# A four-layer graph network on one core: matmuls of no use in TensorE's waits at the start, and a new order table

## The chip, the cores and the metric

The kernel runs on one core of a Trainium2 chip. The core's engines work side by side, each through its own queue in order: TensorE (PE; its weight loads are the row PEld), VectorE (DVE), ScalarE (ACT), GpSimd (POOL) and SyncE (SP, which here only issues DMAs). Time is the device's microseconds from launch to end. Of the kernel before there are three timed runs, with a median of 3752.26 us (3751.09 to 3758.95), and one profiled execution.

## The reference

32 graphs, each of N = 512 nodes with D = 256 features in float32 and a symmetric 0/1 adjacency with ones on the diagonal, go through four graph layers. Ahead of each layer stands a norm without weights and a ReLU, around it a residual sum:

```python
for layer in (L0, L1, L2, L3):
    h = maximum(layernorm(x), 0)
    x = x + layer(h, adj)
```

- Layer 0 is graph attention with 4 heads of 64: `Wh = h @ W`, scores `leaky_relu(e_src[i] + e_dst[j])` masked by the adjacency, softmax over j, `alpha @ Wh`, ELU.
- Layer 1 is the same with one head of 256 and a softmax over the other axis.
- Layer 2 has scores `(h * a) @ h.T`, leaky ReLU, mask, softmax, times `h`.
- Layer 3 is a transformer block: q, k and v, 8 heads of 32 under the mask, an output projection, a norm, a feed-forward part of 256 x 1024 x 256 with ReLU, a norm.

## The kernel before, in words

Nodes are laid in four tiles of 128 partitions. All matmuls take float32. The profile shows each of them as two MATMUL rows, and a transpose (a matmul with the identity, L257) as one.

Nothing is written out in the order in which it runs. `quick_path` records each graph's work as jobs: `plan.dve`, `plan.act`, `plan.matmuls`, `plan.dma` (L214, L235, L257 and L259 are the lines that issue them, whatever the stage, so that stages are told apart by the names of tiles). Each job of a graph has a number in the order of recording, and the table `PLACES` holds one place for each number. Job n of graph b stands at

```python
place = self.number * ROUND + self.table[self.at] if self.place is None else self.place
```

with `ROUND` = 100000 as the distance of two graphs. The table reaches up to 491710, so the work of up to five graphs interleaves: while one is in layer 3, the next are in the layers 2, 1 and 0. `carry_out` (L178) sorts all jobs by place and issues them; each engine's jobs are tied together in just this order ("as planned"). An engine thus never passes over a job that waits. One table serves all 32 graphs: at the start, when the graph ahead is missing, its jobs are missing too, and nothing takes their room.

`aside(place)` (L141) gives the jobs that follow a fixed place: the late loads of weights on POOL, and a few one-off steps.

On its way a graph passes these tiles, in TensorE's terms:
- layer 0: transposes of `h` into `ps_t`, `ps_wh` (128x264), the small transpose `ps_sp`, whose result goes to DRAM (`rows_d`) and comes back spread over all partitions (`rows`, 1 MB); then four heads. For each, VectorE makes four `p` (128x512) from `rows`, and TensorE does 16 matmuls of 128x65 into `ps_o`; VectorE then divides (`rt`, `o`). `p` has six buffers.
- layer 1: `ps_t`, `ps_wh` (128x258), `ps_sp`, 16 matmuls of 128x256 (`ps_o1` in the code, `ps_o` in the profile).
- layer 2: `ps_t`, `ps_e`, the transposes `ps_y`, `ps_o2` (128x257).
- layer 3: `ps_t3` (in the profile `ps_t`), `ps_v`, `ps_qk`, then eight rounds of `ps_s` (scores), exp on ScalarE, the product `p` with the mask on VectorE, `ps_ct` and `ps_to`; then `ps_wo`, `ps_t3`, `ps_f1`, `ps_f2` (both `ps_f` in the profile).

The mask of a graph (`m`) is transposed by four DMAs (`mT`). In PSUM the layers 0 to 2 take the two buffers of `ps_a`, layer 3 the two of `ps_b` (two banks each) and `ps_ct`, `ps_to`.

Of the kernel before, what the change touches and what calls it, by code (L numbers as in the profile page):

```python
# [16 lines left out]
OP = mybir.AluOpType  # L17
AX = mybir.AxisListType

P = 128  # L20
# [36 lines left out]
class Part:  # L57


    def __init__(self, home, rows, index, steps=()):  # L60
        self.home, self.rows, self.index, self.steps = home, rows, index, steps
# [61 lines left out]
class Plan:  # L123
# [6 lines left out]
        tensor_copy=(1,), tensor_scalar_max=(1,), tensor_scalar_mul=(1,),  # L130
    )

    def __init__(self, tc, table):
        self.tc, self.nc, self.table = tc, tc.nc, table
        self.jobs = []

    def graph(self, number):

# [11 lines left out]
    def put(self, engine, takes, ends, outs, ins, call, port=False, moves=None):  # L150

        j = Job()
        place = self.number * ROUND + self.table[self.at] if self.place is None else self.place
        j.place = (place, self.at)
        self.at += 1
        j.engine, j.takes, j.ends, j.call, j.port, j.moves = engine, takes, ends, call, port, moves
        j.after, j.homes = [], []
        before = set()
        for part, writes in [(p, True) for p in outs] + [(p, False) for p in ins]:
            h = part.home  # L160
            r0, r1 = int(part.rows.min()), int(part.rows.max())
            i0, i1 = int(part.index.min()), int(part.index.max())
            if in_psum(part):
                i0, i1 = 0, 1 << 20
            for k, w, a0, a1, b0, b1 in h.uses:
                if (w or writes) and k is not j and a0 <= r1 and r0 <= a1 and b0 <= i1 and i0 <= b1:
                    before.add(k)
            h.uses.append((j, writes, r0, r1, i0, i1))
            if h not in j.homes:
                j.homes.append(h)  # L170
                h.left += 1
        for k in before:
            assert k.place < j.place, "out of order"
            k.after.append(j)
        self.jobs.append(j)
        return j
# [61 lines left out]
    def load(self, tile, source, behind):  # L238
# [7 lines left out]

        return self.put("POOL", 1.0, 0.1, [], [], call)

    def matmuls(self, takes, *calls):

        real = lambda x: x.real() if isinstance(x, Part) else x

        def call():
            made = []
            for c in calls:
                if len(c) == 3:
                    made.append(self.nc.tensor.transpose(*map(real, c)))  # L257
                else:
                    made.append(self.nc.tensor.matmul(*map(real, c[:3]), start=c[3], stop=c[4]))  # L259
            return made  # L260

        outs = [c[0] for c in calls]
        ins = [x for c in calls for x in c[1:3] if isinstance(x, Part)]
        return self.put("PE", takes, takes + 0.2, outs, ins, call)
# [6 lines left out]
def in_psum(x):  # L271
    return isinstance(x, Part) and x.home.kind.tag.startswith("ps")


def width(args):
# [4 lines left out]

ROUND = 100000
PLACES = [
    19807, 0, 43241, 57619, 64598, 73580, 81389, 88138, 134062, 235662, 143142, 287307, 285553, 232853, 15635,
    15811, 28841, 27985, 23993, 15811, 30374, 30229, 32369, 32370, 32370, 32446, 32844, 48496, 34324, 44230,
    44177, 46695, 46041, 50344, 54161, 54792, 54792, 54792, 51041, 51777, 57310, 57310, 57310, 57738, 57738,
    57832, 57739, 58104, 61341, 61341, 67966, 61898, 61898, 67567, 69254, 72469, 69482, 77323, 74000, 76325,
    79818, 78024, 78024, 80713, 80713, 80714, 82170, 88138, 93984, 93675, 88138, 100363, 101562, 103520,
    103520, 103520, 103520, 99026, 98456, 107942, 108892, 114155, 115978, 115979, 116955, 117229, 118109,
    112967, 112266, 118498, 118106, 122333, 124077, 124856, 124856, 126720, 126720, 130323, 126361, 126793,
    124647, 132760, 132760, 132760, 132760, 134221, 134221, 134221, 134221, 134221, 134727, 134221, 156322,  # L290
    140191, 134912, 142057, 169073, 157725, 170057, 172384, 201862, 202787, 205641, 207797, 208539, 176096,
    208573, 211867, 216328, 218484, 218484, 219056, 219056, 219056, 219056, 219056, 218484, 218484, 218484,
    218484, 218485, 227052, 227119, 228253, 219613, 219613, 220424, 224906, 224906, 228631, 223683, 224122,
    224122, 229201, 229201, 232797, 231582, 232020, 232794, 233389, 243904, 244480, 249048, 254893, 242125,
    242231, 243790, 254173, 237217, 238008, 241105, 245079, 237839, 238826, 242604, 256707, 257566, 258334,
    259006, 259006, 259006, 259519, 259519, 259519, 259519, 259519, 392456, 255868, 267182, 259006, 259006,
    259892, 259665, 259006, 259006, 259892, 259665, 266786, 266786, 268621, 269711, 273176, 302934, 273176,
    273176, 273176, 277010, 277447, 281097, 281097, 281195, 281196, 281196, 281682, 281682, 281682, 281682,
    281683, 281196, 281683, 282840, 282840, 284327, 283254, 286775, 286821, 286821, 287236, 288036, 287335,
    282681, 282681, 283122, 282681, 284575, 293213, 293213, 295654, 291792, 291574, 293905, 297714, 297584,  # L300
    297714, 298819, 298819, 297714, 287489, 287489, 290592, 290231, 298206, 300033, 308229, 310297, 310297,
    303799, 303799, 303799, 305379, 305380, 306132, 308300, 312883, 316207, 394029, 437737, 327509, 328548,
    327753, 325228, 328998, 329876, 332238, 330645, 332238, 332502, 332502, 332608, 332717, 364575, 332717,
    332717, 332717, 332717, 332717, 338203, 340406, 340406, 340406, 340407, 340407, 340905, 341309, 341309,
    352943, 347109, 352371, 352371, 353369, 353369, 353417, 354661, 356381, 356381, 356381, 357144, 357399,
    346769, 348254, 348493, 351248, 352029, 352189, 352199, 352199, 352554, 359237, 359237, 359237, 359237,
    364034, 360298, 360301, 360448, 365688, 377452, 366095, 368722, 368232, 374829, 379739, 379671, 380891,
    379672, 382370, 383191, 386847, 392755, 392755, 387818, 392756, 395158, 396303, 407857, 382331, 382331,
    382615, 382634, 388690, 385894, 388773, 389314, 389314, 394131, 390806, 394842, 396200, 401293, 405927,
    398693, 403322, 398865, 403593, 407530, 409955, 410479, 412422, 412422, 408793, 409986, 423530, 354795,  # L310
    408893, 410479, 418263, 418263, 418263, 419191, 419191, 419191, 419191, 419128, 417119, 437177, 437347,
    419191, 420203, 420203, 420203, 420203, 420721, 420203, 420203, 421199, 422452, 422452, 423633, 423633,
    432009, 424134, 424134, 424718, 424718, 424759, 425616, 425916, 425916, 425916, 425916, 426698, 426841,
    426841, 426970, 427475, 430939, 430939, 427202, 428368, 428368, 428368, 429763, 429360, 431209, 431243,
    432263, 432263, 432291, 432540, 430070, 430071, 430071, 430071, 430446, 430071, 431829, 432836, 432836,
    435307, 436332, 440746, 435945, 435945, 436252, 436626, 436626, 437927, 444318, 444318, 444811, 444811,
    444811, 445291, 445291, 445291, 445291, 445447, 445572, 436110, 437653, 437653, 437653, 437653, 437653,
    438770, 440843, 440843, 440843, 440843, 440843, 440872, 442233, 442446, 442446, 442446, 445600, 445600,
    442446, 442446, 445601, 445601, 442446, 442704, 446845, 449648, 449758, 449759, 449759, 454221, 449777,
    450699, 450699, 450699, 450699, 450699, 450699, 491710,  # L320
]


# [1 line left out]
def quick_path(  # L325
# [6 lines left out]
    B, N, D = x.shape  # L332
    NT = N // P
    KD = D // P
# [29 lines left out]
    plan = Plan(tc, PLACES)  # L364

    def new(tag, name, shape, dtype=F32):
        return plan.tile(K[tag], name, shape, dtype)


    ident = const.tile([P, P], F32, name="ident")  # L370
# [14 lines left out]
    w0_t = weight_of(nc, const, w0, "w0_t", 2 * H0)  # L385
# [43 lines left out]
    FULL, HALF = 0.858, 0.4315  # L429
# [372 lines left out]
    bv_w, ps = new("p", "bv_w", [P, N]), new("ps_a", "ps_bv", [P, N])  # L802
# [4 lines left out]

    plan.dve("tensor_scalar_add", b2_r, b2_r, -2.0)
    plan.dve("tensor_add", b1_r, b1_r, ff2b_r)


    for b in range(B):
# [504 lines left out]
```

## Time and profile before

| | us |
|---|---|
| median of three runs | 3752.26 |
| the profiled execution | 3758.1 |
| its span, first to last instruction | 3756.2 |
| PE busy | 3635.0 (97%), 19974 rows |
| DVE busy | 2732.6 (73%) |
| ACT busy | 1803.8 (48%) |
| mean granted TensorE clock | 0.976 |

All that follows is read from that one execution. The page's second part cuts the span in 40 slices of 94 us; a digit is a busy share in tenths, and PEclk is the share of the full TensorE clock that the chip granted:

```profile
PE   4799999999999999999999999999999999999996
PEld 4666766666766666666666666666666666666553
DVE  4577777877777777777787777787777777777653
ACT  1245445555444555444555544555544455544543
POOL 1000000000000000000000000000000000000000
PEclk7599999999999999999999999999999999999998
```

The kernel has a fill of some 300 us, a steady part, and a drain of some 330 us. The view of waits says who waited for whom, in how much time, how often, and how long at most. TensorE's longest:

```profile
PE ps_o L259 <- DVE p L214: 24.6, 9, 10.0
PE ps_t L257 <- ACT h L214: 17.6, 2, 14.8
PE ps_t L257 <- ACT n L214: 12.5, 3, 5.0
PE ps_n L1277 <- DVE least L1273: 8.2, 1, 8.2
PE ps_bv L259 <- issue: 7.3, 1, 7.3
PE ps_ct L259 <- DVE p L214: 6.3, 6, 1.3
PE ps_t L257 <- DVE mc L214: 5.7, 1, 5.7
PE ps_sp L257 <- ACT rt L214: 5.5, 5, 1.4
```

### The profile page before, as it was taken

What the parts mean: (1) busy time and instruction counts of PE and PEld (TensorE: products, weight loads), DVE (VectorE), ACT (ScalarE), POOL (GpSimd) and SP (SyncE); (2) the same over time, 40 slices, a digit from 0 to 9 for tenths busy, and PEclk for the clock granted to TensorE, in tenths of its full rate; (3) what the DMA queues carried; (4) which work ended last, traced back from release to release, by engine and by line L of the source; (5) the groups of instructions that cost most, each with busy time, mean ns of one, the idle gap of its engine ahead of it and who ended that gap; (6) DMA issues with size and microseconds to landing.
All of it is one profiled execution on the core that took longest, in us unless ns stands there. A gap on an engine that the chain in (4) does not pass through costs nothing.

```text
span 3756.2 us, 51774 instructions
## 1 busy us (share of the span) xinstructions
PE 3635.0 (97%) x19974; PEld 2366.4 (63%) x19974; DVE 2732.6 (73%) x6267; ACT 1803.8 (48%) x3393; POOL 11.1 (0%) x25
## 2 busy tenths in 40 slices
PE   4799999999999999999999999999999999999996
PEld 4666766666766666666666666666666666666553
DVE  4577777877777777777787777787777777777653
ACT  1245445555444555444555544555544455544543
POOL 1000000000000000000000000000000000000000
PEclk7599999999999999999999999999999999999998
DMA  4111111111111111011111111111111111100000
GB/s 120 57 32 33 36 49 46 43 42 36 29 49 46 43 49 36 23 47 47 49 43 38 40 29 49 46 43 49 29 29 49 46 43 49 38 29 27 15 9 11
DMA packets 152349, 152.72 MB, mean 41 GB/s; under 512 B 87840, under 2 KB 122144, under 8 KB 148000
## 3 DMA queue, kind: packets, MB, share of 16 engines
q1 hardware_dynamic: 149632, 144.35, 13.8%
q0 software_dynamic: 1216, 3.94, 0.3%
q8 instruction: 159, 2.61, 0.3%
q10 hardware_dynamic: 1248, 1.05, 0.1%
q14 instruction: 94, 0.77, 0.1%
HBM read 114.57 MB, written 17.96 MB: 35 GB/s over the span
## 4 chain that ended last, share of the span: by engine, by line
PE 95%; DVE 3%; ACT 1%; DMA 1%; issue 1%; SPq 0%; ACTq 0%; DVEq 0%
PE ps_o L259 25%; PE ps_f L259 24%; PE ps_s L259 7%; PE ps_ct L259 7%; PE ps_wh L259 6%; PE ps_qk L259 6%; PE ps_to L259 6%; PE ps_e L259 4%; PE ps_t L257 4%; PE ps_v L259 3%; PE ps_wo L259 3%; DVE p L214 1%; PE ps_y L257 1%; DVE st L214 0%; DMA mT<-m 0%
## 5 line engine op out<-in xcount | busy, mean ns | idle before, releaser
L259 PE MATMUL ps_o<-wh,p 128*128 128x65 f32 (+1 forms) x5120 | 750.5, 303 | 30.2 <-DVE p L214 24.6
L259 PEld LDWEIGHTS ps_o<-wh,p 128*128 128x128 f32 x5120 | 705.6, 200 | 102.7 <-issue 60.5
L214 DVE TENSOR_TENSOR p<-p,m 128x2048 f32<-128x2048 f32 x256 | 582.7, 2286 | 29.7 <-ACT p L214 29.6
L214 ACT ACTIVATE p<-ps_s 128x1024 f32<-128x1024 f32 x512 | 501.2, 1022 | 208.1 <-PE ps_s L259 205.3
L259 PE MATMUL ps_f<-tT,ff_t 128*128 128x512 f32 x1024 | 462.7, 602 | 1.7 <-ACT tT L214 1.7
L259 PE MATMUL ps_f<-ff_t,f 128*128 128x256 f32 x2048 | 461.0, 379 | 0.0
L259 PEld LDWEIGHTS ps_f<-ff_t,f 128*128 128x128 f32 x2048 | 381.9, 190 | 64.0 <-issue 15.3
L214 DVE SCALAR_TENSOR_TENSOR p<-rows,rt,mT 128x512 f32<-128x512 f32 x512 | 370.1, 735 | 16.7 <-DMA mT<-m 16.7
L214 ACT ACTIVATE h<-x,shift,rstd 128x256 f32<-128x256 f32 x512 | 268.6, 595 | 152.8 <-PE ps_o L259 106.3
L259 PEld LDWEIGHTS ps_f<-tT,ff_t 128*128 128x128 f32 x1024 | 189.4, 192 | 229.3 <-issue 188.7
L259 PE MATMUL ps_s<-qk 32*128 32x512 f32 x2048 | 294.2, 640 | 1.3 <-ACT qk L214 0.8
L259 PE MATMUL ps_ct<-p,v 128*32 128x512 f32 x2048 | 272.0, 603 | 9.3 <-DVE p L214 6.3
L214 ACT ACTIVATE f<-ps_f,ff1b_c 128x512 f32<-128x512 f32 x256 | 164.8, 682 | 235.7 <-PE ps_f L259 235.7
L259 PE MATMUL ps_to<-p,ones 128*32 128x512 f32 x2048 | 266.6, 592 | 0.0
L259 PE MATMUL ps_qk<-h3T,wqkv_t 128*128 128x512 f32 x512 | 239.1, 594 | 0.0
L259 PE MATMUL ps_o<-h,p 128*128 128x257 f32 x1024 | 239.0, 385 | 0.0
L259 PEld LDWEIGHTS ps_o<-h,p 128*128 128x128 f32 x1024 | 190.1, 191 | 51.5 <-issue 26.0
L214 DVE BATCH_NORM_STATS2 st<-x 128x6 f32<-128x256 f32 x512 | 195.6, 415 | 6.8 <-DMA x<-in_x_dram 4.7
L214 ACT ACTIVATE rstd<-mv,eps 128x4 f32<-128x4 f32 x192 | 56.4, 294 | 298.6 <-DVE mv L214 286.0
L257 PE MATMUL ps_t<-ident,h 128*128 128x128 f32 x1024 | 172.6, 281 | 25.0 <-ACT h L214 17.6
L259 PEld LDWEIGHTS ps_s<-qk 32*128 32x128 f32 x2048 | 81.3, 182 | 164.6 <-ACT y L214 78.0
L257 PEld LDWEIGHTS ps_t<-ident,h 128*128 128x128 f32 x1024 | 130.8, 145 | 85.2 <-issue 52.3
(131 smaller groups left out, 4322.9 us busy)
## 6 DMA issues: line engine op xcount, KB each, us to landing
adj<-in_adj_dram SPq DMA_DIRECT2D x32, 1024.0 KB
rows<-rows_d SPq DMA_DIRECT2D x32, 1024.0 KB
x<-in_x_dram SPq DMA_DIRECT2D x32, 512.0 KB
rows<-rows_d SPq DMA_DIRECT2D x32, 512.0 KB
out_dram<-y SPq DMA_DIRECT2D x32, 512.0 KB
inv<-in_d SPq DMA_DIRECT2D x32, 256.0 KB
ff_t<-in_L_gnn_W_dram POOLq DMA_DIRECT2D x2, 1024.0 KB, 12.5
mT<-m SPq DMA_TRANSPOSE x128
```

The costliest lines, as they stand in the source:

```text
L214: return [getattr(unit, method)(*map(real, args), **{k: real(v) for k, v in kw.items()})]
L257: made.append(self.nc.tensor.transpose(*map(real, c)))
L259: made.append(self.nc.tensor.matmul(*map(real, c[:3]), start=c[3], stop=c[4]))
```

## The change

A new list `WARM` holds 17 places, each with a number of products, 78 in all. At each of these places a job of TensorE is put in, which multiplies the identity with 256 columns of a weight, again and again, into a tile `ps_warm` of the kind `ps_b`. Nothing reads the tile. By their places they stand around the work of the first graph in the layers 0 to 2 (and that of the graphs 1 and 2 in layer 0): 15 ahead of graph 0's heads of layer 0, then 3, 4 and 3 between these heads, 8 ahead of graph 1's first transposes, 16 ahead of graph 1's heads and 3 between its first two, and the rest ahead of graph 2's transposes and `ps_wh`, and around `ps_e` and `ps_y` of graph 0; the last 2 stand between `ps_t3` and `ps_v` of graph 0.

The table `PLACES` is replaced as a whole; it reaches up to 478083. `Plan` gets an argument `own`, a table for a graph of its own, which is left empty, and a method `accumulate`, which is not called.

```diff
-    def __init__(self, tc, table):
-        self.tc, self.nc, self.table = tc, tc.nc, table
-        self.jobs = []
+    def __init__(self, tc, table, own=()):
+        self.tc, self.nc, self.table, self.own = tc, tc.nc, table, dict(own)
+        self.jobs, self.number = [], None
...
-        place = self.number * ROUND + self.table[self.at] if self.place is None else self.place
+        place = self.number * ROUND + self.own.get(self.number, self.table)[self.at] if self.place is None else self.place
...
+    def accumulate(self, out, in_):
+
+
+        def call():
+            return [self.nc.gpsimd.dma_start(out.real(), in_.real(), accum_op=OP.add)]
+
+        return self.put("POOL", 1.0, 0.1, [out], [in_], call, moves=5.0)
...
 PLACES = [
-    19807, 0, 43241, 57619, 64598, 73580, 81389, 88138, 134062, 235662, 143142, 287307, 285553, 232853, 15635,
...
+    4941, 0, 45989, 55878, 52736, 53088, 65883, 75806, 126827, 257141, 153885, 318759, 211656, 217633, 19570,
...
+WARM = [
+    (86598, 15), (103134, 3), (109304, 4), (117054, 3), (143513, 8), (186598, 16), (203134, 3), (243513, 8),
+    (253820, 2), (255983, 5), (262834, 2), (270581, 1), (273590, 2), (279107, 2), (281742, 1), (286598, 1),
+    (341669, 2),
 ]
...
+    for place, products in WARM:
+        plan.aside(place)
+        ps = new("ps_b", "ps_warm", [P, KD, N])
+        plan.matmuls(HALF * products, *((ps[:, 0, :D], ident, w0_t[:, 0, :D], True, True) for _ in range(products)))
```

What the new table moves, read from the order of the instructions on each engine:
- SP: of each graph's four mask transpositions three now stand ahead of the store to `rows_d` (before: two), the fourth behind it, and the load of `rows` behind all four (before: ahead of the fourth).
- TensorE, in the steady part: runs of products of one kind are longer (69 a graph, before 81). Some `ps_wh` of layer 1 that alternated with eight rows of a head now stand in runs of four products; half of layer 0's last head comes after layer 3's second `ps_t3`; a few `ps_f2` come ahead of the last `ps_f1`.
- VectorE: the first head's four `p` are the third, fifth, first and fourth made (before: the first, fourth, third and second), in the order in which TensorE takes them.
- TensorE, at the start: `ps_wh` of graph 2 comes ahead of `ps_o1` of graph 0 (before: after its first eight rows).

## The prediction

> **What bounds the kernel now.** I read the stretches first: one period of the steady part, then the stages of the first 304 us, cut where TensorE changes its work.
>
> ```profile
> core 0: us, PE busy (x) PEld busy (x) DVE busy (x) ACT busy (x) POOL busy (x), PEclk, DMA share, GB/s
> 303.75:415.13 111.38, 111.38 (x626) 72.40 (x625) 84.96 (x196) 56.22 (x107) 0.00 (x0) 1.00 0.15 41
> ```
>
> One graph costs 111.38 us, TensorE is busy throughout at the full clock, VectorE for 85 us. 32 x 111.38 = 3564 of the 3756.2 us; the other 192 lie in the fill and the drain. The fill (length, TensorE's busy time and rows, granted clock, DMA share, GB/s):
>
> ```profile
> 0.00:34.78 34.78, 8.64 (x25) 0.92 0.89 251
> 34.78:69.29 34.51, 28.80 (x128) 0.50 0.08 29
> 69.29:95.96 26.67, 8.06 (x29) 0.69 0.30 82
> 95.96:112.72 16.76, 14.47 (x64) 0.50 0.16 60
> 112.72:138.40 25.68, 23.29 (x90) 0.50 0.06 21
> 138.40:151.90 13.50, 2.23 (x10) 0.50 0.05 10
> 151.90:190.15 38.25, 30.56 (x111) 0.72 0.28 79
> 190.15:219.19 29.04, 25.59 (x154) 0.91 0.06 19
> 219.19:240.23 21.04, 19.94 (x70) 0.82 0.06 13
> 240.23:303.75 63.52, 63.52 (x429) 1.00 0.18 52
> ```
>
> TensorE idles 78.7 us of this, nothing after 240.23, and until 138 it runs mostly at half clock. The same 32 rows of one head of layer 0 show the price in the timeline:
>
> ```profile
> 62.22 7.06 PE L259 MATMUL ps_o<-wh,p 128*128 128x65 f32 x32 [2.86 <-DVE mv L214]
> ...
> 198.43 3.68 PE L259 MATMUL ps_o<-wh,p 128*128 128x65 f32 x32
> ```
>
> A head is 7.06 us cold, 3.6 warm. The drain (59 us lost, from 3422 on) gets no products and keeps its sequence of layers: I leave it at nothing, +-3.
>
> **The rule and the row.** The Trainium skill (TensorE: Matmul & The Clock Gate, "What's actually happening") says that the clock halves after one idle window of some 3.4 us and is full again after one busy window, windows running freely. By it the heads from 36.7 to 69.3, busy almost without a gap, would have warmed themselves, and only the waits would matter. The trace says otherwise (windows as its clock records are cut):
>
> ```profile
> 45.94:49.35 3.41, 3.41 (x18) 0.50 0.02 5
> 76.66:80.07 3.41, 3.10 (x10) 0.50 0.39 77
> 80.07:83.48 3.41, 2.52 (x12) 1.00 0.00 0
> ...
> 199.54:202.95 3.41, 3.01 (x27) 1.00 0.02 5
> ...
> 213.19:216.60 3.41, 2.54 (x21) 1.00 0.03 6
> 216.60:220.02 3.42, 3.42 (x18) 0.50 0.43 156
> ```
>
> At 45.94 a fully busy window of 128x65 heads stays at half; at 80.07 the clock returns after 128x256 products and transposes. From start to start a warm 128x256 row takes 216 ns and a 128x512 row 429, 0.83 ns a column; a head row of 65 columns should stream for 54 ns but takes 112. Counted so, windows that kept a full clock streamed 0.42 or more, those that lost it 0.35 or less; those that regained it 0.80 or more, none with 0.72 did. These are estimates from the trace's rows. Hence heads (0.48) hold a warm clock but cannot raise a cold one, and a wait of over some 0.7 us ahead of heads can lose it. By the rule the products before the heads would be wasted; by the rows the 3 or 4 between heads decide.
>
> **The products.** 78 of 128x256: two rows each, 2 x 216 ns = 0.43 us, 33.7 us in all warm, twice that cold. They run where the timeline has PE waiting: 15 (6.5 us) in the 10.0 us before graph 0's heads, 16 (6.9) in the 8.9 before graph 1's, 8 (3.5) in the 7.3 before ps_bv, 15 in the waits of 5.7, 2.8 and 2.7 around 144 to 152. There they cost nothing warm; cold, 15 take 12.9 us against 11.2. Nothing else waits for ps_warm; ps_b is free until layer 3 at 219.
>
> **The fill, stage by stage** (before, then forecast):
> 1. To the first head's start, 36.68. The fourth mask transposition now goes ahead of the rows load on SP's queue instead of behind; the chain of waits ends there on 5.41 us of DMA mT from 28.34, of which the transposition's own packets are the last 1: 1.0 us earlier. But the first head's second product wants VectorE's fifth p, not its fourth: 0.7 later. Gain 0.3. The 15 products start at 24.8 and end at 31.3; head 0 starts at 36.4: five idle us, the clock is lost.
> 2. Heads of graph 0, 32.6 us. Head 0 cold 7.0; three products cold 2.6, of which one window must catch 1.8 us to reach 0.8 (I put that at 0.7). Then warm heads are paced by VectorE: reciprocal and multiply 0.6, two p of 0.68, say 2.0 with latency, while products run. 7.0 + 2.6 + 3.6 + 2 x (2.0 + 3.6) = 24.4, plus 2.0 for the 0.3 in which head 1 is cold too: 26.4. Gain 6.2.
> 3. To graph 1's heads, 28.6 us: VectorE, ScalarE and DMA (norm, masks, rows), none touched by the clock. Rows last gains 1, fifth p and two small steps ahead lose 1. Gain 0; again 2 to 3 us idle before the heads, so cold.
> 4. Two heads, 14.9 us: 7.0 + 2.6 + 3.6 + 1.2 = 14.4. Gain 0.5.
> 5. To the end of graph 1's heads, 25.7 us: warm content is transposes 0.9, ps_wh 3.6, heads 7.1; with the copies' and VectorE's 2.1, 13.7; 1.5 more for a late clock. Gain 10.5.
> 6. To the end of layer 1's ps_o (161.4), 23.0 us: 13.5 of it is VectorE's and ScalarE's chain, unchanged; ps_wh of graph 2 now stands ahead of ps_o (+0.9), which falls from 9.5 to 6.9. Gain 0.9.
> 7. Layer 2 of graph 0, 169.34 to 198.5: transposes -1.0, first ps_e -1.7, further ps_e -1, head 5.6 to 3.5, ps_o 8.4 to 7.0: gain 6.
> 8. To 219.19: 2.0 cold (the head of 5.06 should take 3.6). To 240.23: 16.5 us of content took 21.0, of which 1.1 is a wait: 2.5. Then no idle time before, none expected after.
> Sum: 0.3 + 6.2 + 0.5 + 10.5 + 0.9 + 6 + 2.0 + 2.5 = **29 us**.
>
> **The new table in the steady part.** The same matmuls in another order. Priced pair by pair with the start-to-start times of before, a graph's TensorE work is 111.1 to 111.2 against 111.33: runs of one kind fall from 81 to 69, but the costly switches between whole array and 32-row or 32-column products stay at 27. What goes is ps_wh alternating with heads (273 instead of 217 ns, some five times). 0.2 x 28 graphs = **6 us**. The page's other engines get nothing new.
>
> **Sum.** 29 + 6 = 35 off the profiled 3758.1 (span 3756.2): 3723. The median of three is 3752.3, 5.8 below that execution: **3717**.
>
> **Rivals.** (a) *The clock never falls from graph 0's heads on.* Stage 2 is then 4 x 3.6 + 3 x 2.0 = 20.4 (gain 12.2), stage 4 9.2 (5.7), stage 5 13.7 (12), stage 8 5.9: 43, with the table 49: 3703. Against it: the five idle us after 31.3. For it: were the rows to land sooner, the products would reach the heads.
> (b) *The products do not bring the clock back.* Stage 2 is 4 x 7.05 + 10 x 0.86 = 36.8 (+4.2), stage 4 +1.8, stage 6 +2, stage 7 and 8 -4: a loss of 4 against 6 of the table: 3750, no change. For it: heads never rise alone. Against: ps_bv and transposes raised it in one window at 80.07.
> (c) *Slower: VectorE takes over the attention loop of every graph.* Between the first and the last ps_ct of a graph TensorE has 33.2 us of work in the new order, before 35.1; VectorE, from first to last p, 31.9 after 30.6. Its lead shrinks from 4.5 to 1.3 us, at the sixth p I count 0.6 left (ScalarE's two exps 2.1, p 2.2, other work ahead). If waits there reach 1.25 us a graph, 28 x 1.25 eats the 35; at 2.0 it is 3752 + 56 - 35 = 3773. For it: VectorE's 98% in 260 to 290 of before. Against: each p still fits.
>
> **Chances.** Main 0.55, (a) 0.25, (b) 0.10, (c) 0.10 (in three of ten of its cases it only eats a part). 0.2%, or 7.5 us, is what can be told from no change: faster 0.86, same 0.06, slower 0.08. The range runs from (a) less the drain's 3 and the 4 us of cold and waiting that it leaves in stage 8, 3696, to (b) less ten for a clock that returns in stage 5, 3740.
>
> **What would show it.** Granted clock 0.5 for head 0 of graphs 0 and 1 and 1.0 from their second head on; graph 0's last head ending at 62 to 64, t3 of layer 3 near 193, the first ps_s near 211, the period at 111.1 to 111.3 with TensorE busy all of it. Wrong if: the clock is 1.0 at 40 (a), heads of 7 us with products between (b), a wait of ps_ct on p in every period (c), or if a wait of graph 0's own chain stands where the clock's loss stood, so that stage 5 keeps its 25 us.

## The result, and the profile after

The changed kernel takes **3717.19 us** (median of four runs, 3714.46 to 3724.77) against 3751.68 (four runs of before): ratio 0.9902, 95% interval 0.9889 to 0.9915. The forecast was 3717, with 3696 to 3740 around it. The profiled execution took 3724.77 us (span 3722.8) and is the slowest of the four; the same kernel, profiled once more (after_again below), took 3716.54. Both are needed below.

The page (busy time of the span, and the granted clock in 40 slices of 93 us):

```profile
span 3722.8 us, 52235 instructions
PE 3638.5 (98%) x20130; PEld 2376.4 (64%) x20130; DVE 2742.9 (74%) x6267; ACT 1813.4 (49%) x3393; POOL 11.1 (0%) x25
...
PEclk8899999999999999999999999999999999999998
```

PE has 156 rows more, two for each of the 78 products, and the first slice is at 0.8 of the clock where it was at 0.7. The stretches of the start, cut where TensorE changes its work as before (length, busy time and rows of each engine, granted clock, DMA share, GB/s):

```profile
core 0: us, PE busy (x) PEld busy (x) DVE busy (x) ACT busy (x) POOL busy (x), PEclk, DMA share, GB/s
0.00:34.70 34.70, 15.68 (x55) 11.42 (x55) 14.59 (x43) 7.42 (x18) 11.08 (x25) 1.00 0.88 268
34.70:63.96 29.26, 27.50 (x149) 25.84 (x150) 13.42 (x30) 0.50 (x2) 0.00 (x0) 0.71 0.04 15
63.96:90.44 26.48, 19.92 (x78) 15.01 (x77) 12.50 (x37) 6.96 (x18) 0.00 (x0) 0.87 0.38 101
90.44:104.63 14.19, 13.30 (x70) 12.57 (x71) 6.07 (x13) 2.08 (x4) 0.00 (x0) 0.64 0.10 36
104.63:118.05 13.42, 12.67 (x92) 11.01 (x92) 8.56 (x23) 2.89 (x9) 0.00 (x0) 1.00 0.00 0
118.05:132.21 14.16, 10.48 (x42) 7.88 (x42) 11.89 (x30) 6.49 (x12) 0.00 (x0) 0.88 0.22 57
132.21:164.70 32.49, 27.75 (x126) 21.15 (x125) 18.25 (x52) 10.60 (x29) 0.00 (x0) 0.92 0.27 90
164.70:191.18 26.48, 25.61 (x154) 22.21 (x154) 17.90 (x58) 6.50 (x18) 0.00 (x0) 0.91 0.00 1
191.18:209.94 18.76, 17.98 (x72) 11.93 (x73) 14.21 (x37) 12.92 (x23) 0.00 (x0) 1.00 0.18 49
209.94:275.07 65.13, 65.13 (x444) 41.31 (x444) 59.04 (x122) 34.13 (x64) 0.00 (x0) 1.00 0.15 48
275.07:386.12 111.05, 111.05 (x626) 72.54 (x626) 85.34 (x195) 56.53 (x108) 0.00 (x0) 1.00 0.14 42
```

The first ps_f1 starts at 275.1 instead of 303.8, the clock is at half only in pieces, and one graph costs 111.05 us with TensorE busy throughout. The steps of the forecast, each measured between the same marks (us; "again" is the other execution of the same kernel):

| step | before | forecast | after | again |
|---|---|---|---|---|
| 1, to the first head | 36.7 | 36.4 | 36.0 | 36.7 |
| 2, heads of graph 0 | 32.6 | 26.4 | 27.9 | 24.8 |
| 3, to graph 1's heads | 28.6 | 28.6 | 27.8 | 27.8 |
| 4, its first two heads | 14.9 | 14.4 | 12.9 | 13.2 |
| 5, to the end of its heads | 25.7 | 15.2 | 13.4 | 13.4 |
| 6, to the end of layer 1's ps_o | 23.1 | 22.2 | 21.2 | 21.2 |
| to layer 2's transposes | 7.8 | 7.8 | 6.8 | 6.8 |
| 7, layer 2 to its last ps_o | 29.2 | 23.2 | 28.2 | 23.2 |
| 8, to layer 3's ps_t | 20.6 | 18.6 | 16.9 | 16.9 |
| 8, to the first ps_s | 21.0 | 18.5 | 18.8 | 18.8 |
| to the first ps_f1 | 63.5 | 63.5 | 65.1 | 65.1 |
| 28 graphs | 3118.6 | 3113 | 3110.5 | 3109.6 |
| the last three, and the end | 333.9 | 333.9 | 337.3 | 337.1 |

Start 28.7 (29 forecast), steady part 8.1 (6 forecast), drain 3.4 lost (0 forecast, +-3): 33.3 between the two profiled executions. TensorE's waits:

```profile
PE ps_t L265 <- ACT h L214: 21.0, 10, 14.3
...
PE ps_o L267 <- DVE p L214: 9.1, 7, 3.5
...
PE ps_ct L267 <- DVE p L214: 7.0, 8, 1.4
```

ps_o for p fell from 24.6 to 9.1 us, mostly since products stand in the same time. ps_ct for p is 7.0 in 8 over the whole run, all of it after 3440 us, so VectorE is late nowhere in the steady part.

One thing is needed for reading these numbers: over 49 runs the kernel before falls into two groups, 26 runs around 3750.6 us and 23 around 3758.6, with none between 3754 and 3756, and its profiled execution (3758.1) is of the upper one.

### The profile page after: what moved, and what is told of

The parts are those of the page before. It is cut to its first block, busy times and chain, and to the rows that moved or that the text cites. A ratio compares the mean times of both kernels' runs of the same rounds, so it can differ in the third digit from the quotient of the medians.

```text
span 3722.8 us, 52235 instructions
## 1 busy us (share of the span) xinstructions
PE 3638.5 (98%) x20130; PEld 2376.4 (64%) x20130; DVE 2742.9 (74%) x6267; ACT 1813.4 (49%) x3393; POOL 11.1 (0%) x25
## 3 DMA queue, kind: packets, MB, share of 16 engines
q1 hardware_dynamic: 149632, 144.35, 13.4%
## 4 chain that ended last, share of the span: by engine, by line
PE 94%; DVE 3%; DMA 1%; ACT 1%; issue 0%; SPq 0%; ACTq 0%; DVEq 0%
PE ps_o L267 24%; PE ps_f L267 24%; PE ps_s L267 7%; PE ps_ct L267 6%; PE ps_wh L267 6%; PE ps_qk L267 6%; PE ps_to L267 6%; PE ps_t L265 4%; PE ps_e L267 4%; PE ps_v L267 3%; PE ps_wo L267 3%; DVE p L214 1%; DMA rows<-rows_d 1%; PE ps_y L265 1%; DVE st L214 0%
## 5 line engine op out<-in xcount | busy, mean ns | idle before, releaser
L267 PE MATMUL ps_o<-wh,p 128*128 128x65 f32 (+1 forms) x5120 | 723.8, 298 | 9.5 <-DVE p L214 9.1
L267 PEld LDWEIGHTS ps_o<-wh,p 128*128 128x128 f32 x5120 | 679.5, 194 | 76.7 <-issue 37.3
L214 DVE TENSOR_TENSOR u<-ps_f,n 128x512 f32<-128x512 f32 x64 | 44.3, 692 | 237.4 <-PE ps_f L267 237.4
L214 DVE BATCH_NORM_STATS2 st<-x 128x6 f32<-128x256 f32 x512 | 204.3, 415 | 9.1 <-DMA x<-in_x_dram 4.7
L265 PEld LDWEIGHTS ps_t<-ident,h 128*128 128x128 f32 x1024 | 120.3, 142 | 93.5 <-issue 52.3
```

The source lines that it names most:

```text
L214: return [getattr(unit, method)(*map(real, args), **{k: real(v) for k, v in kw.items()})]
```

## The experiments

Medians of four or more runs; the ratio is to the runs of before on the same chip. Stage 5 is the stretch from graph 0's transposes of layer 1 to the end of graph 1's heads.

| kernel | us | ratio (95%) | first ps_f1 | stage 5 |
|---|---|---|---|---|
| table_alone | 3733.97 | 0.9951 (0.9937-0.9965) | 285.3 | 14.4 |
| products_alone | 3750.76 | 0.9988 (0.9980-0.9996) | 293.2 | 21.9 |
| no_between | 3726.76 | 0.9930 (0.9917-0.9943) | 279.6 | 14.3 |
| between_only | 3723.61 | 0.9922 (0.9909-0.9936) | 275.5 | 13.4 |
| narrow_between | 3729.98 | 0.9937 (0.9924-0.9951) | 280.8 | 13.9 |
| five_between | 3721.51 | 0.9914 (0.9899-0.9929) | 274.0 | 13.4 |
| after_again | 3714.79 | 0.9887 (0.9872-0.9903) | 268.0 | 13.4 |
| alternate | 3739.58 | 0.9963 (0.9949-0.9976) | 290.8 | 14.8 |
| late_copy | 3739.96 | 0.9955 (0.9941-0.9968) | 291.6 | 15.7 |
| both_undone | 3740.12 | 0.9962 (0.9948-0.9976) | 291.4 | 15.4 |
| held | 3709.25 | 0.9883 (0.9868-0.9898) | 262.4 | 13.4 |
| held_drain | 3704.44 | 0.9858 (0.9843-0.9873) | 262.5 | 13.4 |

**The two halves of the change.**

```diff
 table_alone:     -WARM = [ (86598, 15), ... ]
                  +WARM = []
 products_alone:  PLACES of before;
                  +WARM = [(100362, 15), (114154, 3), (122332, 4), (132759, 3), (149999, 8), (200362, 16), ...]
```

> The new table with an empty WARM, so no products. Theory of the prediction (the products are worth some 29 us in the fill, the table some 6 to 8 in the steady part): 3742 to 3748 us, period 111.05, granted clock 0.5 from 29 us on as before, graph 0's heads at half clock and ending at 64 to 69, first ps_f1 near 302. Rival, that the new sequence does it all and the products are decoration: 3717, first ps_f1 near 275.

> The table of before with the same 78 products ahead of the same pieces of work. Theory of the prediction: 3722 to 3730 us, period 111.38 as before, first ps_f1 at 275 to 281. Rival, the sequence does it all: 3750 or more, first ps_f1 near 304.

Neither theory holds. The table alone takes half a per cent, far more than the 6 to 8 us that I gave it, and the products alone 0.12%. In table_alone the period is 111.05 and 28 graphs take 3109.5; its other gain is in the start, 18.4 us to the first ps_f1 without one product. That is against the one profiled execution of before. The mean of table_alone's runs (3735.2) lies 19.1 us below the mean of before's 27 runs on that chip (3754.3); less the 9.0 of the period and plus the 2.9 that it loses in the drain, some 13 us are left for the start (an estimate). Two of its stretches (graph 0's heads, then stage 5), and stage 5 of products_alone:

```profile
34.16:70.02 35.86, 28.56 (x128) 27.68 (x128) 13.42 (x30) 0.50 (x2) 0.00 (x0) 0.50 0.03 13
...
113.52:127.97 14.45, 14.16 (x90) 12.04 (x90) 8.65 (x23) 2.89 (x9) 0.00 (x0) 0.87 0.00 0
```

```profile
105.45:127.30 21.85, 19.45 (x91) 17.07 (x92) 8.51 (x22) 2.78 (x10) 0.00 (x0) 0.63 0.04 15
```

Graph 0's heads stay cold without products, as forecast. But stage 5 falls from 25.7 to 14.4 by the table alone: the clock there is full from 117.4, behind a window of graph 0's own transposes and ps_wh that streamed 0.89. With products and the old table the stage keeps 21.9 us and its clock is back only at 121.7. The forecast had given this stage's gain to the products. To the first ps_f1 the halves add up (18.4 + 10.6 against 28.7 together). At the end they do not: products_alone loses 4.0 us in the drain, where it has before's table and no products. The mean clock alone says little: products_alone has 0.985 of it and takes longer than table_alone with 0.980, since a clock that is kept up in a wait brings nothing by itself.

**What in the products counts.** no_between drops the 3, 4, 3 and 3 between heads, between_only keeps just these, narrow_between gives them 65 columns. In the expectations "the rule" is that any busy window of TensorE brings the clock back; "the rows" is the reading of the prediction, by which the streamed share counts: the columns that pass in a window, at 0.83 ns each when warm and 1.67 when cold, over its length.

```diff
 no_between:     -(103134, 3), (109304, 4), (117054, 3), (203134, 3)
 between_only:   +WARM = [(103134, 3), (109304, 4), (117054, 3), (203134, 3)]
 narrow_between: +(103134, 6, 65), (109304, 8, 65), (117054, 6, 65), (203134, 6, 65)
                 +(ps[:, 0, :wide], ident, w0_t[:, 0, :wide], True, True)
```

> The changed kernel without the 3, 4 and 3 products between graph 0's heads and the 3 between graph 1's; the other 65 stay. By the rows (a window must stream 0.75 or more to raise the clock, heads of 65 columns stream 0.5): clock 0.5 through the heads of both graphs, graph 0's heads still end at 64 to 65 since the cold products cost what they bring there, graph 1's heads end 8 to 11 us later than 118; 3724 to 3728. By the rule that one busy window brings the clock back: it is back during head 0, and the time is 3713 to 3717.

> The changed kernel with only the 13 products between the heads (3, 4, 3 and 3); the 65 others are gone. By the rows: the clock is up within graph 0's heads and after graph 1's head 0 (100 or so), but transposes and ps_wh ahead of graph 1 run cold in part and the layers 1 and 2 of graph 0 lose the clock at their waits as before: 3728 to 3738. If the products ahead of the heads and in the other waits are of no use: 3717.

> The changed kernel with the 3, 4, 3 and 3 products between the heads made narrow: 6, 8, 6 and 6 products of 128x65 in their place, about as long in time when cold. By the streamed share (0.5 in a window of them, 1.0 in a window of wide ones): they bring no clock back, as if they were left out, 3724 to 3728, graph 0's heads end at 69 to 71. By a rule that counts a busy TensorE: the clock comes back as with the wide ones, 3714 to 3719, graph 0's heads end at 61 to 64.

no_between came out at the time of the rows' theory, though graph 0's heads end at 70.8, not 64 to 65: between cold heads TensorE waits 2.2 us for VectorE's p, which I had left out. between_only falls between the two theories (3728 to 3738, and 3717): 13 products bring 10 of the 17 us that 78 bring on top of the table. narrow_between decides between rule and rows. Its timeline from graph 0's head 0 (start, length, instruction), then a clock window in it and the one after which the clock came back:

```profile
43.35 2.76 PE L267 MATMUL ps_warm<-w_t,ident 128*128 128x65 f32 x12
45.91 7.03 PE L267 MATMUL ps_o<-wh,p 128*128 128x65 f32 x32
```

```profile
42.46:45.87 3.41, 3.41 (x18) 3.41 (x18) 2.24 (x5) 0.00 (x0) 0.00 (x0) 0.50 0.00 0
...
73.18:76.59 3.41, 3.41 (x9) 2.69 (x9) 2.40 (x5) 1.06 (x1) 0.00 (x0) 0.50 0.00 0
```

From 37 to 73 us TensorE is busy without a pause, at half clock, with 18 rows of 65 columns in a window or across its edges (a share of 0.51); one window of 9 wide rows, at 73.2, raises it. Narrow products are as good as none (3730.0 against 3726.8).

**Where the edge of the window falls.**

```diff
 five_between: -(103134, 3), (203134, 3)
               +(103134, 5), (203134, 5)
 after_again:  no edit
```

> The changed kernel with 5 products instead of 3 between heads 0 and 1 of graph 0 and of graph 1 (4.3 us cold). If three failed at 42 us only because the edge of a clock window cut the burst (1.2 and 1.6 us, where 1.8 in one window are needed), five always leave enough in one: head 1 of graph 0 runs at full clock in every execution, graph 0's heads take 24 to 25.5 us instead of 27.9, 3713 to 3716. If the phase of the windows doesn't matter: head 1 stays cold and the time is 3717 to 3719.

> The changed kernel unaltered, on the chip of the next three, so that they stand beside it: 3714 to 3722.

Two executions of the same code show it best; first the changed kernel as profiled, then again:

```profile
42.09 2.87 PE L267 MATMUL ps_warm<-w_t,ident 128*128 128x256 f32 x6
44.75 6.93 PE L267 MATMUL ps_o<-wh,p 128*128 128x65 f32 x32
```

```profile
43.16 2.56 PE L267 MATMUL ps_warm<-w_t,ident 128*128 128x256 f32 x6
45.56 3.72 PE L267 MATMUL ps_o<-wh,p 128*128 128x65 f32 x32
```

The three products between head 0 and 1 fail in one and succeed in the other. In the first a clock window ended at 43.32 and cut the burst in 1.2 and 1.4 us; in the second a window ran from 41.86 to 45.27 and held 2.1 us of it. That is 3.1 us in graph 0's heads. Layer 2 gives 5.0 more (28.2 and 23.2 us): the clock falls there at 159.4 in the first execution and not in the second, so that most of 24 head rows (4.60 and 2.89 us) and ps_o are cold in the one and warm in the other. The rows of ps_o:

```profile
164.70 9.60 PE L267 MATMUL ps_o<-h,p 128*128 128x257 f32 x32
```

```profile
160.03 7.17 PE L267 MATMUL ps_o<-h,p 128*128 128x257 f32 x32
```

Less 1.0 that the second execution loses elsewhere (0.7 to the first head, 0.3 in graph 1's heads), this is the difference of 7 us at the first ps_f1. In five_between the five products did warm head 1:

```profile
42.98 4.58 PE L267 MATMUL ps_warm<-w_t,ident 128*128 128x256 f32 x10
47.35 3.78 PE L267 MATMUL ps_o<-wh,p 128*128 128x65 f32 x32
```

But cold they take 4.58 us where VectorE leaves 2.2: head 1 starts 4.2 us after head 0 ends, and the kernel gained nothing (3721.5; the 3713 to 3716 were missed).

**What in the table shortens stage 5.** Three edits of table_alone, for the first graphs only:

```diff
+def moved(jobs):
+    return [jobs.get(n, place) for n, place in enumerate(PLACES)]
 alternate:   +plan = Plan(tc, PLACES, {0: moved({150: 209310, 151: 209350}), 1: moved({92: 109320})})
 late_copy:   +plan = Plan(tc, PLACES, {1: moved({86: 105110, 90: 105109, 88: 105971})})
 both_undone: both, 1: moved({86: 105110, 90: 105109, 88: 105971, 92: 109320})
```

> table_alone with one more edit, for the start only: graph 0's third to sixth ps_wh product of layer 1 and graph 1's third head of layer 0 alternate again as in the kernel before (ps_wh x2, head rows of 4, ps_wh, 4, ps_wh, 8, ps_wh x4), where the new table has runs of four products and sixteen. No products without use. If the long run is what brings the clock back at 117 in table_alone (window of 0.75 or more): the clock stays at half to 130 or later, graph 1's heads of layer 0 end 7 to 11 us later than there (D to E 22 to 25 us, not 14.4), 3738 to 3745. If that stage's gain comes from VectorE, DMA or fewer waits: 3734 and 14 to 16 us.

> table_alone with one edit, for graph 1 only: VectorE takes one p ahead of its o and one p ahead of graph 0's copy of h1T, as the kernel before does, where the new table has o, copy, p, p. No products without use. In the kernel before, TensorE waits 0.5 us for that o in the middle of its eight transpositions and 0.8 us for the copy ahead of ps_wh, and the clock windows there streamed 0.70 and 0.72; in alternate, with the early copy, 0.85. If the copy's place alone decides: the clock stays at half to 130, D to E 21 to 26 us, 3741 to 3747. If the run of four ps_wh products (3.8 us cold) is enough by itself: the clock is back one window later at most, D to E 15 to 17, 3733 to 3738.

> late_copy and alternate together: the late copy and the alternation of ps_wh with head rows, at the start only; all else as in table_alone. If the new table gets the clock back in that stage by these two, either of which is enough: windows of 0.63 to 0.74, the clock at half to 130 or later, D to E 21 to 26 us, 3742 to 3749. If something else in the table does it: 14 to 16 us, 3733 to 3740.

All three kept the short stage (14.8, 15.7, 15.4 us, one trace each): neither the long runs of ps_wh nor VectorE's order around its copy is the cause, alone or together. late_copy was also meant to bring back the wait of 0.83 us that before has ahead of ps_wh, and did not, so this wait stays untested. Their totals are some 6 us above table_alone, nearly all of it in layer 2 (29.8 to 30.1 us, there 25.2), far from the edits; I did not follow that. Two windows of before, and the one of both_undone after which the clock rose:

```profile
114.20:117.62 3.42, 2.52 (x8) 1.90 (x9) 2.66 (x5) 0.20 (x1) 0.00 (x0) 0.50 0.00 0
117.62:121.03 3.41, 3.41 (x15) 3.13 (x13) 0.00 (x0) 0.37 (x1) 0.00 (x0) 0.50 0.00 0
```

```profile
116.90:120.31 3.41, 3.33 (x11) 2.55 (x12) 2.65 (x5) 0.83 (x2) 0.00 (x0) 0.50 0.00 0
```

Counted by columns as in the prediction, these streamed 0.63, 0.72 and 0.81 of their time. Before has two waits in this place, 0.48 us in the middle of the transposes and 0.83 us ahead of ps_wh (VectorE copies the half that was transposed last); both_undone has only the first, since in the new table VectorE copies the half that was transposed first. 0.83 us are 0.24 of a window, more than is missing. The two traces with the old table have both waits; all twelve with the new table have the full clock before the middle of the stage. So the wait ahead of ps_wh is my best reading; it was argued from these rows and not tried by itself.

The phase of the windows has a part in it too. The last eight rows of ps_wh in this stage, in before (126.48 to 130.2) and in products_alone (119.21 to 122.4), whose sequence is the same:

```profile
124.44:127.86 3.42, 3.42 (x14) 3.15 (x14) 1.11 (x3) 0.00 (x0) 0.00 (x0) 0.50 0.00 0
127.86:131.27 3.41, 2.37 (x6) 1.35 (x4) 1.63 (x6) 0.97 (x5) 0.00 (x0) 0.50 0.00 0
```

```profile
118.33:121.74 3.41, 3.41 (x12) 2.94 (x12) 2.25 (x7) 0.00 (x0) 0.00 (x0) 0.50 0.00 0
```

In before an edge cuts these rows, the windows streamed 0.66 and 0.63, and the clock stayed at half; in products_alone most of them fall into one window, it streamed 0.84, and the clock came back. By these two traces, the stage turns on where the edges fall as long as the old table stands. Had before's window of 0.72 been full enough, the stage's last 17.4 us would have run at full clock, up to some 8 us less (an estimate): as much as lies between the two groups of before's times. No execution of the lower group was profiled, so this is not shown; but some of the 11 us that stage 5 gains by the table may be the bad luck of the one execution of before.

**Filling what is left.**

```diff
 held:       +(86598, 24), (103134, 4), (117054, 4), (143513, 13), (149999, 2), (186598, 22), (203134, 4),
             +(243513, 13), (253820, 3), (255983, 6), (262834, 3), (268505, 1), (279107, 3), (285039, 2), (286598, 2)
 held_drain: held with (86598, 26), (186598, 24),
             +(3311044, 5), (3411044, 11), (3418254, 2), (3457834, 3), (3459376, 2), (3511044, 11), (3518254, 2)
```

> The changed kernel with the waits that are left filled as well: 24 ahead of graph 0's heads, 22 ahead of graph 1's, 4 between heads, 13 ahead of the transposes of graphs 1 and 2, 2 ahead of ps_bv, and 1 to 3 more at graph 0's ps_e, ps_y and the others. If the clock then never falls below full from 23 us to layer 3: graph 0's heads take 20.5 to 22 us, the two of graph 1 9 to 10, layer 2 24 to 25; 3700 to 3706. If filling the waits does not hold the clock, or the products come in the way of the heads: 3714 to 3722.

> held with 26 and 24 products ahead of the two graphs' heads (there the window with the wait for the second p streamed 0.36 and lost the clock), and 45 products in the drain: 5, 11 and 11 ahead of the last transpositions of the graphs 29 to 31, 2 ahead of ps_f1 of the graphs 30 and 31, 3 and 2 ahead of the last graph's first two ps_s. If the clock is then full from 23 us to the drain, graph 1's two heads take 9 to 10 us instead of 12.0; if the products hold it in the drain, ps_f1 of the last two graphs take 14 us instead of 16 and first ps_f1 of graph 28 to that of graph 31 285 to 288 us instead of 290.6: 3699 to 3705. If the fill is as in held and the drain gains nothing: 3708 to 3711.

The stretches of graph 0's heads, graph 1's first two and layer 2 in held:

```profile
36.74:58.46 21.72, 20.16 (x151) 18.76 (x152) 12.09 (x28) 0.50 (x2) 0.00 (x0) 1.00 0.01 2
84.79:96.81 12.02, 12.02 (x71) 11.30 (x71) 4.75 (x11) 2.08 (x4) 0.00 (x0) 0.72 0.00 1
138.24:161.57 23.33, 22.22 (x117) 17.39 (x117) 15.29 (x38) 5.67 (x13) 0.00 (x0) 1.00 0.35 119
```

Graph 0's heads run at full clock for the first time, 21.7 us instead of 27.9. The clock falls once between 30 us and layer 3, at 87.4: behind the first product of graph 1's first head TensorE waits 0.89 us for the second p, and the window with this wait streamed 0.36. The two heads took 12.0 us instead of the 9 to 10 expected, and held missed its 3700 to 3706 by 3 us. In held_drain, which has 36 products in the drain and not the 45 that its expectation names, graph 1's heads are warm (first line), and from the 29th graph's ps_f1 to the last's, TensorE runs at 0.99 of the clock, where held has 290.58 us at 0.96:

```profile
87.61:96.91 9.30, 8.94 (x71) 8.41 (x71) 4.75 (x11) 2.08 (x4) 0.00 (x0) 1.00 0.01 2
...
3373.33:3661.64 288.31, 270.64 (x1357) 155.80 (x1356) 170.35 (x345) 131.00 (x218) 0.00 (x0) 0.99 0.04 13
```

In this one execution graph 0's head 0 lost the clock instead (24.4 us for its heads; the window from 34.9 to 38.3 streamed 0.25). At 3704.4 us held_drain beats both kernels, by 10 us against the changed one on the same chip.

## Why the prediction was right, and where it was not

- **The time** and the size of the start's gain (29, measured 28.7) were right. Half of the reasons were not, and that the sums met is in part luck: the new table and the products together gave in stage 5 what the products were to give alone, and the 2 us that the steady part brought above the forecast stand against 3.4 lost in the drain.
- **Step 5** failed as the prediction put it: it gave the 10.5 us to heads kept warm by products. The runs show 11.2 us from the table alone; the products add 1.0. The term at fault is that of the table in the start: I had priced it by the steady part and put it at almost nothing there (0.3 gained in step 1, 0 in step 3, 0.9 lost in step 6). What the table does in stage 5 was not isolated: the wait of 0.83 us ahead of ps_wh is the likely cause, and the phase of before's windows may have a part in the 11.2.
- **Step 2**: that three cold products bring the clock back with 0.7 was sound, with the condition named (1.8 us in one window): it failed in the profiled execution, and succeeded in after_again, between_only and products_alone, which have the same three products. Where it succeeded the step took 24.8 in the changed kernel, forecast 24.4. Without products the table makes this step 34.5 us, so they are worth 6.6 to 9.7 there.
- **Step 7**, 6 us, came in one execution (23.2) and not in the other (28.2): a wait ahead of 24 head rows left a window at 0.37, and the ps_o behind took 9.6 us instead of 7.2. The terms of this step add up to 7.2, not 6. Steps 6 and 8 gave about 2.5 more than forecast, of which 0.8 is a slip in step 6: its own terms (9.5 to 6.9, less 0.9) make 1.7, not 0.9, and 1.9 was measured; half a head that now runs ahead of ps_f1 took 1.6 back.
- **The period**: 0.29 us a graph over the 28 (0.325 in the one shown), not 0.2. The term that I named, ps_wh alternating with heads, measured 0.27 (3.81 to 3.55 us a graph); ps_f1, ps_e and ps_t gained 0.1 each, ps_y and ps_sp lost 0.1 each.
- **The drain**: 3.4 lost, just outside the +-3. The cause is open: table_alone loses 2.9, but products_alone, with the old table, loses 4.0.
- **From profile to median** I took 5.8 off, since that execution lay so much above. It is of the upper group of before's times; the changed kernel's profiled execution lies 7.6 above its own median, so the two profiles compare as the medians do. That was luck, not argument.
- **Rivals**: (a), a clock that never falls, isn't what the change does (half clock from 36.5 and 35.0), but held shows that its 20.4 us for graph 0's heads was well priced (21.7). (b) is what happened to head 1 of graph 0 in the profiled execution. (c) is refuted: TensorE is busy 111.05 of 111.05 us.
- **Rule against row**: the Trainium skill (TensorE: Matmul & The Clock Gate, "What's actually happening") has the clock full after a busy window; narrow_between, busy for 36 us at half clock, contradicts that for 65-column products. The same section says that windows run freely, so that the point of transition varies from run to run; the two executions of the changed kernel agree, and here it is worth 7 us, heads and layer 2 together.

## What to carry to other kernels

Where TensorE waits for other engines at the start, products of no use paid here when they were wide (256 columns), fitted into the wait even at half clock, and ended where the real work began; narrow ones (65 columns) did nothing. Before such an edit is credited, run the other half of the change alone: here the new sequence, priced at 6 us, brought about half of the gain. And take two profiled executions where a clock is in play, since the same code differed by 7 us in the part under study.

## What the runs showed of the hardware

Over the first 235 us of all 14 traces there are some 850 clock windows of 3.41 us. With the streamed share counted from rows and columns (an estimate: 0.83 ns a column at full clock, 1.67 at half), the 60 windows after which the clock rose had 0.75 or more, and none of 239 that stayed cold had over 0.74; the 60 after which it fell had 0.39 or less, and none of 493 that kept it (after 30 us) less than 0.37. The upper bound is not that sharp: with a row's columns counted at its end and not at its start, the lowest share after which the clock rose is 0.72, and the highest that stayed cold 0.77. Heads of 65 columns stream 0.51 cold, between the two bounds: they hold whichever clock they meet. That before's times fall in two groups 8 us apart, with nothing between, fits such bounds: in the 27 runs beside table_alone the mean granted clock is 0.978 in the lower group and 0.976 in the upper, some 15 to 20 us more at half clock, which cost about half as much where TensorE is busy. Which window of before does it was not seen, as only one execution of it was profiled; the one of 0.72 in stage 5 is a candidate.
